# Two scan layers of a state-space stack: Softplus, step size products and their stores moved to later slots, GpSimd's units of B to other slots

## The chip, the core and the metric

The kernel runs on one core of a Trainium2 chip. Its engines are TensorE (PE in the profile), VectorE (DVE), ScalarE (ACT) and GpSimd (POOL); SyncE (SP) issues all transfers. Each engine works through its own queue in order. The metric is the device time of one execution in microseconds, the median over several runs.

## The reference

Four layers are applied to an image batch x of shape (8, 48, 48, 96), each as x = x + layer(group_norm(x)). Layer 1 is a band-limited quadratic MLP. Layers 0, 2 and 3 hold a selective scan: with 192 channels and 16 states, along the 2304 pixels in four directions in layers 0 and 3, and along single rows or columns of 48 pixels in layer 2. Layers 0 and 3 compute, per direction,

```python
dts, Bs, Cs = jnp.split(x_dbl, [R, R + N], axis=2)
dts = jnp.einsum('bkrl,kdr->bkdl', dts, dt_projs_weight)
delta = jax.nn.softplus(dts + dt_projs_bias...)
def step(h, inp):
    u, dl, Bv, Cv = inp
    dA = jnp.exp(dl[..., None] * A)
    h = h * dA + (dl * u)[..., None] * Bv[:, :, None, :]
    y = jnp.einsum('bkdn,bkn->bkd', h, Cv)
    return (h, y)
```

and then sum the four directions, normalise, gate with silu(z) and project back.

## The kernel before, in words

The layers run as `ss2d("l0")`, `lines` and `ss2d("l3")`. The MLP of layer 1 is a "guest": its pieces are put between the others' work while `l0` and `lines` run. The two calls of `ss2d` are called the scan layers here, the first and the last one.

**Blocks, slots, turns.** A scan layer has 8 images (jobs), 4 directions (two in row order, two in column order; they run in the order 0, 1, 3, 2) and 5 blocks of pixels, so 20 blocks a job and 160 a layer. Four blocks of a direction have ten rows (480 pixels, called full), one has eight (384). A block is worked off in 8 slots, and two slots make a turn; turns are counted 0 to 3. A slot holds one half of the channels and four of the 16 states, spread over 128 partitions and 3 units along the free axis. `ORDER` gives slots 0 to 3 the first half of the channels and slots 4 to 7 the second half, with the groups of states in reverse; so slots 3 and 4 use the same rows of B and C.

**What one unit needs.** `make_da` (L329) is the exponential of step size times A, on ScalarE, two units at a time, into one of two PSUM tiles `da`. `make_dbu` (L305) multiplies the products step size times u by B. `scan` (L337) is the recurrence, two units at a time, on VectorE. `make_hc` (L343) multiplies the three units of a slot by C on GpSimd, and `reduce` (L363, L365) sums over the states on TensorE.

**Who multiplies by B.** `on_pool` gives per slot how many of the three units GpSimd takes (the last ones, with B from SBUF); VectorE takes the others, with B copied to PSUM by ScalarE in `copy_b` (L286), a single buffer. Where GpSimd has all three units no copy is made. Where slot 3 has a copy, slot 4 shares it.

**The order of a turn.** The loop over turns issues, on every engine's queue, in this order: scan of pair 0; product with C of the slot before; VectorE's B products of slot at+2; exponentials of pair 1; GpSimd's B products of slots at+2 and at+3; reduction; scan of pair 1; exponentials of pair 2; copy of B and VectorE's B products of slot at+3; reduction; `aside(at)`; product with C of the turn's first slot; exponentials for the next turn's pair 0; scan of pair 2; copy of B of slot at+4; `aside(at + 1)`. So each B product is made a turn before its scan: slot 0 and 1 of the next block in turn 3.

**Asides.** `aside(at)` issues the loads and the work of `stage1` that are due at a slot. For block b, counted in slots from the start of the block two before it, `stage1` does: projection to the raw step sizes, B and C; their copy to `bcl` (L724) at slot 1; at slot 3 the store of B and C and the matrix product of the step sizes (L709); at slots 4 and 5 the biased step sizes of the two halves (L713), written to `dds`, a tile with one buffer; then Softplus over both halves in one instruction (L737, with a table load before it and another before the next exponential), the products step size times u on GpSimd (`make_du`, L505, with two small memsets), and per half a store of `dds` to device memory (`store_dd`, L491). In the block before b, the load of each half, replicated to 128 partitions (`load_dd`, L258), stands at slots 3 and 5, and the loads of B and C (`load_bc`, L270) at slots 1, 1, 6 and 7. A load of a half waits for that half's store. L713 of the next block waits for both stores.

In `lines` the corresponding steps are others: Softplus stands in the slot 0, and the products and both stores in slot 1, of the block before; the change does not touch it.

**Other work.** The asides also hold the side work of a scan layer (convolution of the next image with its Silu pairs, L593 and L595; normalisation and output of the image before, L609 to L659) and, in the first scan layer and `lines`, the guest.

Of the kernel before, what the change touches and what calls it, by code (L numbers as in the profile page):

```python
# [29 lines left out]
NG = 8  # L30
# [14 lines left out]
FAR = 1e30  # L45
CH = 96

ON_POOL_SS = {2: 1, 3: 3, 5: 1, 6: 1, 7: 3}
ON_POOL_L2 = {4: 3, 6: 3, 7: 3}


# [51 lines left out]
def vss_stack_kernel(ctx: ExitStack, tc: tile.TileContext, i: dict, out: bass.AP):  # L103
# [386 lines left out]
    def store_dd(b, half):  # L490
        nc.sync.dma_start(b.dd[half].rearrange("j (g m) -> g j m", g=3), b.dds[:, half].rearrange("p t m -> p (t m)"))  # L491

    def sizes(b, half):

        return [b.dds[:, half, n, b.at] for n in range(2)]

    def make_room(b, pools):
        b.room = pools["dds"].tile([DH, LEAD + 4 * WMAX], F32, tag="dds", name="dds")
        b.dds = b.room[:, LEAD:LEAD + 4 * b.m].rearrange("p (h t m) -> p h t m", h=2, t=2)

    def make_du(b, u):


        dt, du = [b.dds[:, :, n, b.at].rearrange("p h (r s) -> p h r s", s=SEG) for n in range(2)]
        nc.gpsimd.tensor_mul(du, dt, u)  # L505
        if b.m == b.n:
            at = SEG - 1 if b.rev else 0
            nc.gpsimd.memset(dt[:, :, :, at:at + 1], FAR)
        else:

            far = b.dds[:, :, :, b.came:] if b.back else b.room[:, :4 * b.m].rearrange("p (u m) -> p u m", m=b.m)[:, :, :LEAD + 1]
            nc.gpsimd.memset(b.dds[:, :, :, 0:1] if b.back else b.dds[:, :, :, b.goes:], 0.0)
            nc.gpsimd.memset(far, FAR)


    def ss2d(l, xin, xout, guest=None):
# [185 lines left out]
        def stage1(b):  # L702
            n = b.n
            u, uall = b.view(us[b.job], dirs[b.k][0]), b.view(uss[b.job], dirs[b.k][0])
            got = {}

            def raw(half):
                got["p"] = ps("s1", 1)
                nc.tensor.matmul(got["p"][:, :n], lhsT=wide("dtw", (2 * b.k + half) * DH), rhs=b.bcl[:, :n],  # L709
                                 start=True, stop=True)  # L710

            def biased(half):
                nc.scalar.activation(sizes(b, half)[0], got["p"][:DH, :n], AF.Identity,  # L713
                                     bias=w[f"{l}_dtb"][:, b.k, half:half + 1])

            def s0():
                got["p"] = ps("s1", 1)
                for half in range(2):
                    nc.tensor.matmul(got["p"][:, :n], lhsT=wide("xp", (2 * b.k + half) * NBC), rhs=uall[:, half],  # L719
                                     start=(half == 0), stop=(half == 1))  # L720

            def s1():
                b.bcl = pools["bcl"]
                nc.scalar.copy(b.bcl[:NBC, :n], got["p"][:NBC, :n])  # L724

            def s3():
                nc.sync.dma_start(b.bcd, b.bcl[:2 * NS, :n])
                raw(0)

            def s4():  # L730
                make_room(b, pools)
                biased(0)
                raw(1)

            def s6():
                both = b.dds[:, :, 0, b.at]
                nc.scalar.activation(both, both, AF.Softplus)  # L737

            def du():
                make_du(b, u)  # L740

            def store(half):
                return lambda: store_dd(b, half)

            return {-1: s0, 1: s1, 3: s3, 4: s4, 5: lambda: biased(1), 6: s6, 7: du,
                    NG: store(0), NG + 1: store(1)}

        def so_far(b, half):
            if b.job not in yss:
# [19 lines left out]
        for _ in conv(0, BLKS[:1]):  # L769
            pass  # L770
        scans(dirs, (0, 1, 3, 2), False, ON_POOL_SS, a, pools, ps, stage1, opening, done, side, tail, conv(0, BLKS[1:3]), guest)
        for _ in post(nb - 1, BLKS[:1]):
            pass
# [581 lines left out]
```

## Time and profile before

| | us |
|---|---|
| median of 3 runs | 17278.24 |
| lowest, highest | 17277.93, 17287.99 |
| profiled execution, its time | 17276.01 |
| profiled execution, its span | 17274.2 |

The profile comes from one execution. Its page gives busy time by engine and by group of instructions; the waits name, for the idle time of an engine, the instruction that waited and what it waited for; the timeline lists instructions with start and duration. A row of a group reads: line, engine, operation, output<-inputs, shape, count, then total busy us and mean ns of one, then the idle time before them and its main cause. SPq is SyncE's queue. By layer, in us of busy time:

| stretch | length | PE | DVE | ACT | POOL |
|---|---|---|---|---|---|
| first scan layer, 0 to 5909 | 5909 | 4635.0 | 5241.6 | 4684.1 | 5165.8 |
| `lines`, 5909 to 11854 | 5945 | 4497.7 | 5368.8 | 4921.7 | 4934.8 |
| last scan layer, 11854 to 17274 | 5420 | 3949.9 | 5186.2 | 4291.6 | 5087.6 |

### The profile page before, as it was taken

To read this page: it belongs to the slowest core of one execution; us is meant where nothing else is said; L and a number is where in the kernel's file an instruction comes from. 1 tells how busy PE (TensorE), PEld (TensorE's weight loads), DVE (VectorE), ACT (ScalarE), POOL (GpSimd) and SP (SyncE) were. 2 spreads that over 40 slices of the span, in tenths; PEclk is the share of its full clock that TensorE was granted. 3 is DMA by queue.
4 is the path that set the end of the run, shared out by engine and by line. 5 is a ranking of instruction groups with operands and counts; after the bars stand their busy time and mean duration, and the time that the engine had idled before them with its cause. 6 is when DMAs were issued, how large, how long until landed. Compare 5 with 4: busy or idle time off the path is not lost.

```text
span 17274.2 us, 168621 instructions
## 1 busy us (share of the span) xinstructions
PE 13082.7 (76%) x53740; PEld 4691.8 (27%) x53740; DVE 15796.7 (91%) x9680; ACT 13897.4 (80%) x20972; POOL 15188.2 (88%) x7999
## 2 busy tenths in 40 slices
PE   6778787878787677777777777776777777777776
PEld 1223232333332333233323332221222222222221
DVE  7999999998899799999999999996999999999998
ACT  6878888878787688888888888885878878878876
POOL 7998888988889688888888888887999999999998
PEclk7878888888898789899889998887878878878877
DMA  4555555454555444444444444443545455555454
GB/s 140 177 174 169 177 167 182 168 178 169 171 174 174 134 152 160 162 159 155 156 163 156 158 162 153 156 154 126 176 172 175 173 172 173 175 173 180 168 176 145
DMA packets 887917, 2843.64 MB, mean 165 GB/s; under 512 B 353469, under 2 KB 421789, under 8 KB 760207
## 3 DMA queue, kind: packets, MB, share of 16 engines
q1 hardware_dynamic: 887022, 2832.85, 48.3%
q8 instruction: 423, 6.93, 0.2%
q14 instruction: 472, 3.86, 0.1%
HBM read 2384.40 MB, written 448.17 MB: 164 GB/s over the span
## 4 chain that ended last, share of the span: by engine, by line
ACT 22%; POOL 21%; DVE 19%; issue 15%; DMA 13%; PE 9%; SPq 1%; POOLq 0%; DVEq 0%; ACTq 0%
POOL dbu L343 13%; DVE dbu L337 12%; ACT ps_da L329 8%; DMA dd<-dds 6%; DVE dbu L305 6%; POOL dbu L305 5%; DMA dd<-dd 4%; ACT L329 3%; POOL dds L505 3%; PE ps_y L363 2%; ACT ps_b L286 2%; DMA bc<-bcd 1%; PE ps_side L580 1%; ACT L737 1%; PE ps_s L709 1%
## 5 line engine op out<-in xcount | busy, mean ns | idle before, releaser
L337 DVE TENSOR_TENSOR_SCAN dbu<-ps_da,dbu 128x968 f32<-128x968 f32 (+3 forms) x5760 | 11826.1, 2075 | 889.5 <-ACT ps_da L329 725.5
L343 POOL TENSOR_TENSOR dbu<-dbu,bc 128x1440 f32<-128x1440 f32 (+1 forms) x3840 | 10071.2, 2635 | 1709.2 <-DVE dbu L337 1133.6
L329 ACT ACTIVATE ps_da<-dd,w_l_a 128x484 f32<-128x484 f32 (+3 forms) x11520 | 7417.2, 649 | 2337.4 <-DVE dbu L337 2108.6
L363 PE MATMUL ps_y<-dbu,w_red 128*32 128x480 f32 (+1 forms) x23040 | 4261.4, 656 | 1676.9 <-POOL dbu L343 1643.4
L365 PE MATMUL ps_y<-dbu,w_red 128*32 128x480 f32 (+1 forms) x7680 | 4222.1, 656 | 0.0
L305 DVE TENSOR_TENSOR dbu<-dd,ps_b 128x962 f32<-128x962 f32 (+5 forms) x2720 | 3815.4, 1403 | 318.1 <-ACT ps_b L286 164.0
L305 POOL TENSOR_TENSOR dbu<-dd,bc 128x481 f32<-128x481 f32 (+3 forms) x2080 | 3883.8, 1883 | 4.2 <-DMA bc<-bcd 4.1
L363 PEld LDWEIGHTS ps_y<-dbu,w_red 128*32 128x32 f32 x23040 | 717.6, 118 | 5117.2 <-POOL dbu L343 3585.2
L286 ACT COPY ps_b<-bc 128x482 f32<-128x482 f32 (+3 forms) x2720 | 1449.2, 533 | 270.3 <-DVE dbu L305 211.8
L580 PE MATMUL ps_side<-xpad,w_l_cw 128*128 128x480 f32 (+1 forms) x2880 | 1352.9, 608 | 47.4 <-ACT g_room L1181 17.3
L329 ACT ACT_TABLE_LOAD x993 | 1274.0, 1283 | 17.5
L709 PE MATMUL ps_s<-bcl,square 128*128 128x480 f32 (+1 forms) x1280 | 874.7, 774 | 325.9 <-ACT dds L713 170.8
L359 PE MATMUL ps_y<-big,eye 128*128 128x480 f32 (+1 forms) x960 | 745.0, 865 | 247.1 <-ACT big L760 242.4
L719 PE MATMUL ps_s<-big,square 128*128 128x480 f32 (+1 forms) x1280 | 848.8, 794 | 64.2 <-ACT g_room L1181 18.3
L505 POOL TENSOR_TENSOR dds<-dds,big 96x960 f32<-96x960 f32 (+1 forms) x320 | 706.5, 2208 | 144.5 <-ACT dds L737 144.0
L580 PEld LDWEIGHTS ps_side<-xpad,w_l_cw 128*128 128x128 f32 x2880 | 571.2, 209 | 808.9 <-issue 695.1
L872 PE MATMUL ps_sb<-xpad,square 128*128 128x480 f32 (+1 forms) x1280 | 615.7, 628 | 96.7 <-ACT g_room L1181 42.1
L365 PEld LDWEIGHTS ps_y<-dbu,w_red 128*32 128x32 f32 x7680 | 655.9, 118 | 0.0
L872 PE MATMUL ps_sa<-xpad,square 128*128 128x480 f32 (+1 forms) x1280 | 521.2, 548 | 0.0
L713 ACT ACTIVATE dds<-ps_s,w_l_dtb 96x480 f32<-96x480 f32 (+1 forms) x640 | 405.2, 633 | 126.1 <-DMA dd<-dds 81.3
L760 ACT COPY big<-ps_y 96x480 f32<-96x480 f32 (+1 forms) x640 | 471.7, 737 | 37.3 <-PE ps_y L365 35.9
L915 PE MATMUL ps_sa<-xpad,square 128*128 128x480 f32 (+1 forms) x320 | 243.5, 854 | 322.8 <-ACT g_room L1181 108.9
(250 smaller groups left out, 12475.6 us busy)
## 6 DMA issues: line engine op xcount, KB each, us to landing
dd<-dd SPq DMA_DIRECT2D x512, 1452.0 KB
bc<-bcd SPq DMA_DIRECT2D x1536, 480.0 KB
dd<-dd SPq DMA_DIRECT2D x256, 1440.0 KB
dd<-dds SPq DMA_DIRECT2D x512, 363.0 KB
dd<-dd SPq DMA_DIRECT2D x128, 1164.0 KB
bc<-bcd SPq DMA_DIRECT2D x384, 384.0 KB
dd<-dds SPq DMA_DIRECT2D x256, 360.0 KB
dd<-dd SPq DMA_DIRECT2D x64, 1152.0 KB
```

What stands on the lines that cost most here:

```text
L286: nc.scalar.copy(bps[t][:, :bcs[t][0].shape[1]], bcs[t][0])
L305: engine.tensor_mul(o, du, by.unsqueeze(1).to_broadcast([P, hi - lo, by.shape[1]]))
L329: nc.scalar.activation(da[:, at:at + b.m], b.got[half][:, u % 3, 0, :], AF.Exp, scale=a[:, b.k, ci:ci + 1])
L337: nc.vector.tensor_tensor_scan(db, da, db, 0.0, ALU.mult, ALU.add)
L343: nc.gpsimd.tensor_mul(h, h, bcs.pop(2 * t + sub)[1].unsqueeze(1).to_broadcast([P, 3, n]))
L363: nc.tensor.matmul(y[32 * g:32 * g + 32, :n], lhsT=wc["red"][:, :32], rhs=hc[:, g, b.at], start=False, stop=(slot == 3))
L365: nc.tensor.matmul(y[DH:, :n], lhsT=wc["red"][:, 32:], rhs=hc[:, 2, b.at], start=False, stop=(slot == 3))
L505: nc.gpsimd.tensor_mul(du, dt, u)
L580: nc.tensor.matmul(pu[:, :n], lhsT=flat[:, at:at + P], rhs=xpad[:, r0 + dy:r0 + dy + nr, dx:dx + W], start=(tap == 0), stop=(tap == 8))
L709: nc.tensor.matmul(got["p"][:, :n], lhsT=wide("dtw", (2 * b.k + half) * DH), rhs=b.bcl[:, :n], start=True, stop=True)
L719: nc.tensor.matmul(got["p"][:, :n], lhsT=wide("xp", (2 * b.k + half) * NBC), rhs=uall[:, half], start=(half == 0), stop=(half == 1))
L872: nc.tensor.matmul(got["u", half][:, :n], lhsT=wide("cw", at), rhs=shifted(off), start=(tap == 0), stop=(tap == 3))
```

## The change

Two edits, both for the scan layers alone. In `ON_POOL_SS` the three units of slot 3 and the one unit of slot 2 become three units of slot 1 and one of slot 3. In `stage1` Softplus moves from slot 6 to slot 0 of the block after (`NG` is 8), the products from slot 7 to slot 1 of it, and both stores stand right behind the products, where they stood at slots 0 and 1.

```diff
-ON_POOL_SS = {2: 1, 3: 3, 5: 1, 6: 1, 7: 3}
+ON_POOL_SS = {1: 3, 3: 1, 5: 1, 6: 1, 7: 3}
 ON_POOL_L2 = {4: 3, 6: 3, 7: 3}
...
             def du():
                 make_du(b, u)
-
-            def store(half):
-                return lambda: store_dd(b, half)
-
-            return {-1: s0, 1: s1, 3: s3, 4: s4, 5: lambda: biased(1), 6: s6, 7: du,
-                    NG: store(0), NG + 1: store(1)}
+                for half in range(2):
+                    store_dd(b, half)
+
+            return {-1: s0, 1: s1, 3: s3, 4: s4, 5: lambda: biased(1), NG: s6, NG + 1: du}
```

The instruction counts of the multiplies by B stay as they are on both engines: 15 units a block on VectorE in six instructions, 9 on GpSimd in five. The copies of B fall from six to five a block.

## The prediction

> **What bounds the kernel now.** I read the engine totals first, then the waits of each scan layer, then one block on the timeline of each engine.
>
> ```profile
> PE 13082.7 (76%) x53740; PEld 4691.8 (27%) x53740; DVE 15796.7 (91%) x9680; ACT 13897.4 (80%) x20972; POOL 15188.2 (88%) x7999
> L337 DVE TENSOR_TENSOR_SCAN dbu<-ps_da,dbu 128x968 f32<-128x968 f32 (+3 forms) x5760 | 11826.1, 2075 | 889.5 <-ACT ps_da L329 725.5
> ```
>
> VectorE is nearly full. By windows it is busy 5241.6 of the first scan layer's 5909.0 us and 5186.2 of the last one's 5420.0, so what can be won in these two layers is less than 667 + 234 us. The waits say what part of it ScalarE causes: 297.0 us in the first layer and, in the last one,
>
> ```profile
> DVE dbu L337 <- ACT ps_da L329: 84.5, 105, 3.4
> ```
>
> The transfers cost VectorE next to nothing there, but SyncE's queue waits for them all the time (last layer):
>
> ```profile
> SPq L258 <- DMA dd<-dds: 1563.5, 290, 6.6
> ```
>
> This is the load of the step sizes behind their store. One full block of the last layer, VectorE and then SyncE's queue:
>
> ```profile
> 13061.30 2.17 DVE L337 TENSOR_TENSOR_SCAN dbu<-ps_da,dbu 128x968 f32<-128x968 f32 x1 [1.03 <-ACT ps_da L329]
> 13063.39 1.13 DVE L305 TENSOR_TENSOR dbu<-dd,ps_b 128x962 f32<-128x962 f32 x1
> 13064.43 6.29 DVE L337 TENSOR_TENSOR_SCAN dbu<-ps_da,dbu 128x968 f32<-128x968 f32 x3
> ...
> 13087.37 1.63 DVE L305 TENSOR_TENSOR dbu<-dd,ps_b 128x1443 f32<-128x1443 f32 x1
> 13088.92 2.16 DVE L337 TENSOR_TENSOR_SCAN dbu<-ps_da,dbu 128x968 f32<-128x968 f32 x1
> 13091.00 1.63 DVE L305 TENSOR_TENSOR dbu<-dd,ps_b 128x1443 f32<-128x1443 f32 x1
> 13092.55 4.25 DVE L337 TENSOR_TENSOR_SCAN dbu<-ps_da,dbu 128x968 f32<-128x968 f32 x2
> ```
>
> ```profile
> 13061.48 0.74 SPq L491 DMA_DIRECT2D dd<-dds  x1
> 13062.27 2.15 SPq L270 DMA_DIRECT2D bc<-bcd  x2
> 13064.47 1.98 SPq L491 DMA_DIRECT2D dd<-dds  x1
> 13072.29 0.53 SPq L258 DMA_DIRECT2D dd<-dd  x1
> ```
>
> Times below count from the block's first scan (13061.30). The first store leaves at 0.2, the load that waits for it at 11.0, and VectorE first reads the loaded tile at 26.1 (13087.37, slot 0 of the next block). The next block starts at 33.4. So the chain store, load, product has slack now: the trace's landings put the load's end at 21.7 here (13082.95), 4.4 us early; over the layer's full blocks the median slack is 3.3.
>
> The middle layer, which is not changed, already does what the change brings: products and both stores at slot 1.
>
> ```profile
> 8001.32 1.55 SPq L491 DMA_DIRECT2D dd<-dds  x2
> 8010.92 0.56 SPq L258 DMA_DIRECT2D dd<-dd  x1
> ...
> 8015.71 0.55 SPq L258 DMA_DIRECT2D dd<-dd  x1
> 8020.22 1.66 DVE L305 TENSOR_TENSOR dbu<-dd,ps_b 128x1440 f32<-128x1440 f32 x1 [0.81 <-DMA dd<-dd]
> ```
>
> There the product waits for the load. Store to first use is 18.9 us here; from the first store's issue to the load's last landing the median over that layer's full blocks is 18.4.
>
> **GpSimd's units of B.** VectorE's and GpSimd's counts do not change: 9 units a block on GpSimd, 15 on VectorE, in multiplies of the same three widths. Two things do. Slot 3 now has a copy of B in PSUM and slot 4 shares it, and slot 1 needs none: 320 fewer copies (L286, 0.53 us) in all, 170 us of ScalarE, which is no bound. And VectorE's multiplies move: turn 0 gets slot 2's third unit (1.63 - 1.13 = 0.50) and slot 3's two (1.05 back to back), turn 3 loses slot 1's three (1.55). So the first use of the loaded tile moves from 26.1 to 27.6, and from it to the block's end there remain 7.28 - 1.55 = 5.73 us.
>
> **Softplus.** The same 3.6 us (table 1.28, activation 1.01, table 1.28) goes from turn 3 to turn 0. There VectorE has 8.9 us of scans and multiplies; ScalarE has its copy at 4.4, Softplus done by 6.7, the exponentials of the next turn by 9.3 against a need at 8.9. About even, so I take 0; if its cover is gone (a Silu burst of 3.8 in the same turn) it costs up to 2.9. The page "ScalarE: Activation LUTs" of the Trainium skill, section "What ACT_TABLE_LOAD costs", prices a switch at 2.66 us with its drain. By that the burst would be an estimated 6.3 us and each block 2.7 us longer; the trace of this case shows the activation 0.02 us behind a load of 1.28, so I do not use it.
>
> **Products and stores.** They now follow Softplus in the same turn, and on GpSimd they stand behind slot 0's product with C (L343), which needs VectorE's second scan. That scan ends at 5.2 now and at 5.7 after; 2.72 for L343 makes 8.5; the product and its memsets took 2.17 (13093.85 to 13096.02) in row order: the store leaves at 10.7, as in the middle layer. In column order the product takes 2.70 instead of 1.88 (the group of 256 has a mean of 2.29): 11.5. Before it was 0.2 to 1.4. The stores lose some 10 us of lead; the use is only 1.5 later.
>
> With 18.4 the load lands at 29.1 in row order and 29.9 in column order, against 27.6. VectorE stalls 1.5 and 2.3 us, at the one place where it has nothing else queued. GpSimd's new units of slot 1 wait for the same load, but GpSimd gets there only at about 28 to 30, so nothing is added. Since VectorE then starts the next block late, and the stores hang on that block's second scan, this is a loop: a full block can't be shorter than 29.1 + 5.73 = 34.8 (35.6 in column order), where the block shown takes 33.4.
>
> Why a store takes so long decides all this. The trace's landings show three engines' worth of completions for it, and two stores one behind the other: first landed 9.6 us after issue, second at 14.4. The page "DMA: Bandwidth & Descriptors", section "Why a DMA increments its semaphore by 16 and not by 1", says that a transfer's engines are the largest number up to 16 that divides the slowest dimension on both sides; with 3 and 96 that is 3, which fits. The same page's fit in "Anatomy of one DMA" (2.0 us plus bytes at 436 GB/s) speaks against a stall: 2.8 us for 363 KB and 5.3 for the load, an estimate of 18.8 for the landing, 9 us early, and the sum would be no loss. The rows here say 9.6, and they decide.
>
> **Where dds is written next.** The tile has one buffer. The biased step sizes of the following block (L713) wait for both stores. Now they come at 20.2 (ScalarE's timeline, 13081.53) and wait 38.9 us in the whole last layer; after, they come at 21.8 and the tile is free at 10.7 + 14.4 = 25.1. ScalarE stands for 3.3 us in each block, and behind it stand the exponentials of turn 3, and on TensorE the next projection (L709) and the reductions. The exponentials are there at 25.1 + 0.64 + 1.37 = 27.1, so the scan that should run from 25.5 ends at 29.2, just when the load lands: the two delays overlap and are paid once. Bounds for what is added: 0 when they overlap wholly; 320 x 3.3 = 1056 us when nothing covers the wait. ScalarE is idle 21% of the last layer, about 7 us a block, so I stay near the lower end: 0.4 us a block for bursts that find no room, 128 us. SyncE waits in order for GpSimd's product; behind it are the loads of dd, then the store of B and C and the last two loads of B and C, which have 10 us or more to spare as in the middle layer.
>
> **Sum.** A job has 20 blocks: 13 full ones behind a full one (7 row, 6 column), 3 behind one of eight rows (floor 32.4 to 33.2 against 30.8), one short behind short (+2.4), 3 without loss: 33 us a job, 266 us in the last layer if every block were at its median. Many are longer already (mean 34.5, median 33.3). Taking for each block the larger of its own length in the trace and its floor gives +155 us in the last layer, and in the first, where the median full block takes 35.7, +53. With the 128: 336. ScalarE's 170 us earn nothing in blocks that are set by the load. 17276 us for the profiled execution (span 17274.2) + 336 = 17612, and the median of the runs is 2 higher: 17614.
>
> **Rivals.**
> 1. ScalarE and TensorE jam: the wait at L713 is not covered. For it: in the first layer TensorE is busy 78% and also serves the guest layer, and in-order queues pass on every wait. Against it: the 7 us of idle time. If a third of 3.3 us gets through on top in 320 blocks: +350, 17960.
> 2. Faster. The place is Softplus in turn 3, where ScalarE also had two copies; VectorE's 297 + 85 us of waiting for exponentials would halve: -190, 17090. It decides only if the load lands before 27.6, which needs store to landing under 16.9 us; the middle layer has 18.4, and three engines are three engines. Against it also the 3.3 us at L713.
> 3. Near the edge: without the loads of B and C between the stores they land 1.5 us sooner than in the middle layer; only column blocks stall, and the relief pays part: +80, 17360.
>
> **Numbers.** Forecast 0.57, jam 0.2, edge 0.13, faster 0.1. A measurement of this kernel can tell 0.2%, some 35 us, from no change. Faster by more: 0.09; within: 0.05 (the low end of the edge case); slower: 0.86. The forecast's own range is 17,450 to 17,800; 8 in 10 reach from the edge case to the jam: 17,330 to 17,960.
>
> **What would show it.** Right: a new wait of VectorE's L305 for dd in both scan layers, 1 to 2 us a block; L713 waiting for the stores some 3 us a block; stores issued 10.7 to 11.5 after a block's first scan; full blocks of the last layer at 34.8 to 36; the middle layer at its 5945 us. Wrong: the load's landing before 27.6, or stores that land in less than 9 us; waits for ScalarE growing in turn 0 instead would mean that Softplus, not the load, is what was moved into the way.

## The result, and the profile after

The changed kernel takes 18153.1 us (median of 5 runs, 18137.2 to 18169.5) against 17280.9 us before in the same runs: a ratio of 1.050, with a 95% interval of 1.049 to 1.052. It is 872 us slower where 336 were forecast. The direction and the place were right, the size was not.

Engine totals and three groups of the page of the changed kernel (busy us and mean ns, then idle time before the group and its main cause):

```profile
PE 13157.0 (72%) x53740; PEld 4799.0 (26%) x53740; DVE 15851.6 (87%) x9680; ACT 13760.4 (76%) x20653; POOL 15208.8 (84%) x7999
...
L337 DVE TENSOR_TENSOR_SCAN dbu<-ps_da,dbu 128x968 f32<-128x968 f32 (+3 forms) x5760 | 11863.8, 2077 | 1436.7 <-ACT ps_da L329 1156.7
...
L305 DVE TENSOR_TENSOR dbu<-dd,ps_b 128x962 f32<-128x962 f32 (+5 forms) x2720 | 3823.1, 1406 | 575.7 <-DMA dd<-dd 282.0
...
L713 ACT ACTIVATE dds<-ps_s,w_l_dtb 96x480 f32<-96x480 f32 (+1 forms) x640 | 408.0, 638 | 869.3 <-DMA dd<-dds 764.2
```

VectorE does the same work (15,852 us against 15,797) and waits more. The share named "DMA" before L305 is 282 us, but the waits must be read together: L713 on ScalarE waits 764 us for the stores (before: 81), and what VectorE then waits for exponentials (1157 against 725) is partly that wait handed on. From the first scan of a layer to the first scan of the next (in the last layer: of its last block), the first scan layer went from 5793 to 6272 us, the middle one from 5946 to 5937, the last one from 5359 to 5767: +479, -9, +408. The granted clock of TensorE fell from 0.85 to 0.83, but VectorE's waits for TensorE's side work grew by little (L657: from 55 to 73 us in the first scan layer and from 51 to 58 in the last), too little to be a rival.

The block that the prediction showed, in the changed kernel; it starts at 13617.1. SyncE's queue first:

```profile
13627.80 1.64 SPq L491 DMA_DIRECT2D dd<-dds  x2
13637.70 0.56 SPq L258 DMA_DIRECT2D dd<-dd  x1
...
13642.58 0.56 SPq L258 DMA_DIRECT2D dd<-dd  x1
13643.19 11.25 SPq L270 DMA_DIRECT2D bc<-bcd  x4
```

ScalarE's two rows of the biased step sizes:

```profile
13642.63 0.66 ACT L713 ACTIVATE dds<-ps_s,w_l_dtb 96x480 f32<-96x480 f32 x1 [2.49 <-POOL dbu L305]
...
13645.42 0.66 ACT L713 ACTIVATE dds<-ps_s,w_l_dtb 96x480 f32<-96x480 f32 x1
```

And VectorE at the end of the block:

```profile
13644.58 2.17 DVE L337 TENSOR_TENSOR_SCAN dbu<-ps_da,dbu 128x968 f32<-128x968 f32 x1 [0.64 <-ACT ps_da L329]
13647.35 1.66 DVE L305 TENSOR_TENSOR dbu<-dd,ps_b 128x1443 f32<-128x1443 f32 x1 [0.60 <-ACT ps_da L329]
13648.93 6.29 DVE L337 TENSOR_TENSOR_SCAN dbu<-ps_da,dbu 128x968 f32<-128x968 f32 x3
```

The stores leave 10.7 us after the first scan. The second one has landed at 25.4 (13642.53). Right behind it the second load leaves (13642.58), and ScalarE's L713 starts (13642.63), which stood for 2.49 us; the releaser that the profile names is a GpSimd instruction, but the start follows the store's landing by 0.1 us. The trace has the first load's landing at 13647.23, and VectorE's product starts at 13647.35; here too the row names another releaser, an exponential. The next block starts at 13653.1: 35.9 us where it took 33.3.

### The profile page after: what moved, and what is told of

Its sections match the earlier page's. It is cut to its first block, busy times and chain, and to the rows that moved or that the text cites. A ratio compares the mean times of both kernels' runs of the same rounds, so it can differ in the third digit from the quotient of the medians.

```text
span 18151.3 us, 168013 instructions
## 1 busy us (share of the span) xinstructions
PE 13157.0 (72%) x53740; PEld 4799.0 (26%) x53740; DVE 15851.6 (87%) x9680; ACT 13760.4 (76%) x20653; POOL 15208.8 (84%) x7999
## 4 chain that ended last, share of the span: by engine, by line
DMA 30%; ACT 19%; POOL 14%; DVE 14%; issue 12%; PE 10%; SPq 2%; POOLq 0%; DVEq 0%; ACTq 0%
DMA dd<-dds 16%; DVE dbu L337 9%; POOL dbu L343 8%; DMA dd<-dd 8%; ACT ps_da L329 6%; DVE dbu L305 4%; DMA bc<-bcd 4%; ACT L329 3%; POOL dds L505 3%; POOL dbu L305 2%; PE ps_y L363 2%; ACT ps_b L286 1%; PE ps_side L580 1%; DMA out_dram<-xi 1%; ACT L737 1%
## 5 line engine op out<-in xcount | busy, mean ns | idle before, releaser
L363 PE MATMUL ps_y<-dbu,w_red 128*32 128x480 f32 (+1 forms) x23040 | 4183.2, 654 | 1127.4 <-POOL dbu L343 1122.0
L305 DVE TENSOR_TENSOR dbu<-dd,ps_b 128x962 f32<-128x962 f32 (+5 forms) x2720 | 3823.1, 1406 | 575.7 <-DMA dd<-dd 282.0
L305 POOL TENSOR_TENSOR dbu<-dd,bc 128x481 f32<-128x481 f32 (+3 forms) x2080 | 3895.5, 1883 | 302.8 <-DMA dd<-dd 192.0
L365 PE MATMUL ps_y<-dbu,w_red 128*32 128x480 f32 (+1 forms) x7680 | 4148.0, 654 | 0.0
L363 PEld LDWEIGHTS ps_y<-dbu,w_red 128*32 128x32 f32 x23040 | 761.7, 120 | 4469.9 <-POOL dbu L343 2615.2
L286 ACT COPY ps_b<-bc 128x482 f32<-128x482 f32 (+3 forms) x2400 | 1284.8, 535 | 558.1 <-DMA bc<-bcd 358.8
L709 PE MATMUL ps_s<-bcl,square 128*128 128x480 f32 (+1 forms) x1280 | 932.2, 821 | 1068.0 <-ACT dds L713 885.2
L359 PE MATMUL ps_y<-big,eye 128*128 128x480 f32 (+1 forms) x960 | 784.5, 909 | 431.6 <-ACT big L758 425.2
L713 ACT ACTIVATE dds<-ps_s,w_l_dtb 96x480 f32<-96x480 f32 (+1 forms) x640 | 408.0, 638 | 869.3 <-DMA dd<-dds 764.2
L365 PEld LDWEIGHTS ps_y<-dbu,w_red 128*32 128x32 f32 x7680 | 695.6, 120 | 0.0
L709 PEld LDWEIGHTS ps_s<-bcl,square 128*128 128x128 f32 x1280 | 263.9, 252 | 1598.2 <-ACT dds L713 1193.9
L870 PE MATMUL ps_sa<-xpad,square 128*128 128x480 f32 (+1 forms) x1280 | 521.2, 548 | 0.0
```

Of the source, the lines that this page charges most:

```text
L286: nc.scalar.copy(bps[t][:, :bcs[t][0].shape[1]], bcs[t][0])
L305: engine.tensor_mul(o, du, by.unsqueeze(1).to_broadcast([P, hi - lo, by.shape[1]]))
L363: nc.tensor.matmul(y[32 * g:32 * g + 32, :n], lhsT=wc["red"][:, :32], rhs=hc[:, g, b.at], start=False, stop=(slot == 3))
L365: nc.tensor.matmul(y[DH:, :n], lhsT=wc["red"][:, 32:], rhs=hc[:, 2, b.at], start=False, stop=(slot == 3))
L870: nc.tensor.matmul(got["u", half][:, :n], lhsT=wide("cw", at), rhs=shifted(off), start=(tap == 0), stop=(tap == 3))
```

## The experiments

Eight kernels ran; each was timed beside the kernel before. The ratios are to the kernel before.

**The units alone.** The kernel before with one line changed:

```diff
-ON_POOL_SS = {2: 1, 3: 3, 5: 1, 6: 1, 7: 3}
+ON_POOL_SS = {1: 3, 3: 1, 5: 1, 6: 1, 7: 3}
```

> The kernel before with the changed kernel's units of B alone; Softplus, products and stores stay at slots 6, 7, 8 and 9. The load lands as early as before (about 22 us after a block's first scan), so both the theory of the load and that of the wait at the biased step sizes expect no loss: 17,150 to 17,350. A theory that the units themselves cost the time (VectorE's turn 3 is 1.55 us shorter and no longer covers Softplus; GpSimd's three units of slot 1 in turn 3) expects 0.6 to 2 us a block, 17,450 to 17,900.

Measured: 17522.2 us, 1.014 (1.013 to 1.016). Slower by 240 us, within what the third theory expected and not what the first two did, although the load is early (landed 24.7 us after the first scan, needed at 27.7, medians of the last layer's full blocks). The units are no gain by themselves: with Softplus left in turn 3, that turn has only 7.8 us of VectorE's work to cover it and takes 8.6. VectorE's scans wait 167 us for exponentials in the last layer (before: 85) and 397 in the first (before: 297), while their wait for GpSimd's products with C hardly changes in the last layer (28 against 26), so of the two causes that the third theory named the waits show the first.

**The stage alone.** The changed kernel with the old line for the units.

> The kernel before with Softplus, products and stores moved, the units of B as before. The theory of the load: the loop keeps its landing (30.3 us after the first scan in the last layer), but 7.28 instead of 5.73 us of VectorE's work stand behind it, so a block is 1.5 us longer than in the changed kernel: 18,150 + 480 = 18,600, at least 18,400. If the units were the cause of the loss it would be gone: below 17,500.

Measured: 18643.7 us, 1.079 (1.077 to 1.081); the theory of the load said 18,600. So the units are not the cause of the loss; they save 490 us of what the moved stage costs.

**Two buffers of dds in the last layer.** Memory allows it there alone, since the guest's tiles are gone by then; in the first layer this wasn't tried.

```diff
-                 "dds": pool("dds", 1),
+                 "dds": pool("dds", rooms),
...
-        pools, ps = scan_pools(stack)
+        pools, ps = scan_pools(stack, 1 if guest else 2)
```

> The changed kernel with two buffers of dds in the last scan layer alone, so that the biased step sizes there wait for no store. Theory of the load: it lands as before, the last layer stays within 60 us of its 5831, the whole at 18,090 to 18,170. Theory of the wait at the biased step sizes: the last layer loses 150 us or more, the whole is below 18,000.

Measured: 18154.2 us, 1.051 (1.049 to 1.052), with the last layer at 5759 us against 5767. The wait at L713 is gone and nothing is won. The end of the same block on VectorE shows why (timeline):

```profile
13651.57 6.29 DVE L337 TENSOR_TENSOR_SCAN dbu<-ps_da,dbu 128x968 f32<-128x968 f32 x3
13659.76 1.66 DVE L305 TENSOR_TENSOR dbu<-dd,ps_b 128x1443 f32<-128x1443 f32 x1 [1.89 <-DMA dd<-dd]
13661.33 6.30 DVE L337 TENSOR_TENSOR_SCAN dbu<-ps_da,dbu 128x968 f32<-128x968 f32 x3
```

The scans that came late now run in one go, and VectorE waits 1.89 us for the load instead. In the last layer's waits the load takes the first place, with 314 us where the changed kernel showed 67. The changed kernel first, then this one:

```profile
DVE dbu L337 <- ACT ps_da L329: 309.7, 289, 4.6
...
DVE dbu L305 <- DMA dd<-dd: 66.7, 56, 3.9
```

```profile
DVE dbu L305 <- DMA dd<-dd: 314.1, 113, 6.3
DVE dbu L337 <- ACT ps_da L329: 120.5, 186, 4.4
```

**Quick stores in the changed kernel.** Each store is cut into three transfers of 32 rows.

```diff
-        nc.sync.dma_start(b.dd[half].rearrange("j (g m) -> g j m", g=3), b.dds[:, half].rearrange("p t m -> p (t m)"))
+        for g in range(3):
+            nc.sync.dma_start(b.dd[half].rearrange("j (g m) -> g j m", g=3)[g],
+                              b.dds[32 * g:32 * g + 32, half].rearrange("p t m -> p (t m)"))
```

> The changed kernel with each store split into three transfers of 32 rows, one for each group of 32 partitions; in all three scan layers. If a store is slow because its outer dimension of 3 puts it on three engines, it lands in 3 to 5 us instead of 9.7. Theories of the load and of the wait at the biased step sizes alike: the load lands at about 21 us, both waits of dds are gone, 17,100 to 17,400. A theory that Softplus in turn 0 is what costs the time (exponentials late for turn 1): stays above 17,700. If the stores land as late as before, 18,100 and nothing is learned but that.

Measured: 17144.3 us, 0.992 (0.991 to 0.994). SyncE's queue in the same block, which starts at 12948.6:

```profile
12959.26 2.63 SPq L492 DMA_DIRECT2D dd<-dds  x6
12962.26 0.52 SPq L258 DMA_DIRECT2D dd<-dd  x1
...
12965.65 0.52 SPq L258 DMA_DIRECT2D dd<-dd  x1
```

The load of the first half leaves 3.0 us after the first of the six transfers, where it was 9.9. Each transfer lands about 2.0 us after its issue, the load lands at 20.9 us after the first scan (last layer, median) and is needed at 28.2. The two scan layers together take 11141 us against 12039 with the slow stores: 898 us of the changed kernel are the stores' path.

**Quick stores in the kernel before.** The same edit there.

> The kernel before with the split stores, in all three scan layers. Its two scan layers had 3 us of slack at the load and should not change (5793 and 5359 us from the first to the last block's first scan); the middle layer, which stands at its load, should win as it did with the changed kernel, about 110 us: 17,130 to 17,200. If it comes out as after_16 (17,144), the parts of the change are worth nothing once the stores are quick; if it is above 17,250, they are worth something.

Measured: 17063.0 us, 0.988 (0.986 to 0.989), less than expected and the fastest of all kernels here. The middle layer goes from 5946 to 5830 us; the first and the last one also win a little, 5734 and 5333 against 5793 and 5359, which was not expected. Against this kernel the changed one with quick stores is 81 us slower, so the two edits are worth nothing, and cost a little, once the stores are out of the way (82 us more in the first scan layer, 7 less in the last). Of the 887 us that the change added to the two scan layers 74 remain so, and 813 hang on the slow stores.

**The stage alone with quick stores.**

> stage_only with the split stores: Softplus in a turn 0 in which VectorE has 7.3 us of work instead of 8.9. With the store path out of the way, what is left is ScalarE's burst: exponentials for turn 1 at about 9.3 us against a need at 7.3, 1 to 2 us a block in 320 blocks, less the 0 to 1.1 that turn 3 gets back: 17,250 to 17,700. If the units are needed for nothing but the stores' path: 17,150.

Measured: 17374.4 us, 1.006 (1.004 to 1.007), as expected of ScalarE's burst. Turn 0 of a block of the last layer on VectorE; the block's first scan is the second one of the first row, at 12261.1:

```profile
12259.01 4.23 DVE L337 TENSOR_TENSOR_SCAN dbu<-ps_da,dbu 128x968 f32<-128x968 f32 x2
12263.16 1.13 DVE L305 TENSOR_TENSOR dbu<-dd,ps_b 128x962 f32<-128x962 f32 x1
12264.21 4.23 DVE L337 TENSOR_TENSOR_SCAN dbu<-ps_da,dbu 128x968 f32<-128x968 f32 x2
12269.68 2.17 DVE L337 TENSOR_TENSOR_SCAN dbu<-ps_da,dbu 128x968 f32<-128x968 f32 x1 [1.24 <-ACT ps_da L329]
```

The first scan of turn 1 waits 1.24 us for its exponential, and turn 0 takes 8.6 us, as in the median over the layer's full blocks, where it takes 7.3 in the kernel before with quick stores. This wait has nothing to do with a store: the load lands at 21.4 us and is needed at 27.6 (medians). Units alone cost 256 us in the two scan layers (11408 against 11152), the stage alone with quick stores 321 (11388 against 11067 of the kernel before with quick stores), both with quick stores 74: each edit needs the other, since VectorE's work has to stand where Softplus stands. The units alone were not run with quick stores; their load is 3.0 us early in the median as it is.

**Only the second half's store quick.**

```diff
+        if half == 0:
+            nc.sync.dma_start(b.dd[half].rearrange("j (g m) -> g j m", g=3), b.dds[:, half].rearrange("p t m -> p (t m)"))
+            return
+        for g in range(3):
...
```

> The changed kernel with the store of the second half alone split. The first half's store still takes 9.7 us, so the load of the first half leaves at 21 as before. Theory that this load is slowed by the second store, which stands before it on three engines: it takes 6.6 us instead of 9.2, lands at 28 us after the first scan, where VectorE needs it at 28.2, and most of the loss is gone: 17,250 to 17,500. Theory that only the first store's 9.7 us matter: the load lands at 30 as before, 18,000 to 18,150.

Measured: 17390.6 us, 1.007 (1.005 to 1.008), as the first theory said. SyncE's queue in the same block, which starts at 13105.2 (L492 is the slow store, L495 the three quick ones):

```profile
13115.89 0.74 SPq L492 DMA_DIRECT2D dd<-dds  x1
13116.68 3.94 SPq L495 DMA_DIRECT2D dd<-dds  x3
13125.33 0.54 SPq L258 DMA_DIRECT2D dd<-dd  x1
```

The first load leaves 9.4 us after its store, nearly as in the changed kernel, but it lands 6.7 us after that instead of 9.2 (medians, last layer), at 27.3 against a need at 28.2. With the second store quick 763 of the 1009 us that two quick stores win are gone already. Part of this came through the first half's load, which stands behind the second store; the run does not separate it from the store's own later landing, for which L713 and the second load wait.

**Products ahead of GpSimd's product with C.** In the changed kernel `make_du` moves to slot 0, right behind Softplus; the stores stay at slot 1.

> The changed kernel with the products right behind Softplus at slot 0, ahead of GpSimd's product with C; both stores stay at slot 1. Theory of the loop (first scan, products, store, load, next block): products start at 6.7 instead of 8.5 us in the last layer, and some 0.5 to 1 us earlier in the first, where Softplus itself is later; every block that stands at its load gets shorter by that: 290 + 80 to 160 us less, 17,700 to 17,850. If the loss is not set by when the stores leave, 18,100 or more.

Measured: 17844.9 us, 1.033 (1.032 to 1.035): 308 us faster than the changed kernel, as the loop asks, though less than the 370 to 450 that were expected: the last layer won 199 us instead of 290, the first one 92, within its 80 to 160. The stores leave at 9.5 us in the last layer (11.0 in the changed kernel) and 10.7 in the first (11.5).

Medians over the full blocks of the last layer that are followed by a full block, in us from the block's first scan; the landings are the trace's, "needed" is the end of turn 3's first scan:

| kernel | block | store leaves | load leaves | load landed | needed | turns 0 to 3 |
|---|---|---|---|---|---|---|
| before | 33.3 | 1.4 | 12.2 | 22.9 | 26.2 | 7.3, 9.4, 7.3, 9.3 |
| changed | 36.4 | 11.0 | 21.2 | 30.3 | 30.3 | 9.3, 9.5, 8.8, 8.8 |
| two buffers of dds | 36.3 | 10.8 | 21.2 | 30.3 | 28.2 | 9.3, 9.5, 7.3, 10.3 |
| products at slot 0 | 34.9 | 9.5 | 19.3 | 28.4 | 28.6 | 9.3, 9.5, 7.3, 8.4 |
| second store quick | 34.3 | 11.1 | 21.0 | 27.3 | 28.2 | 9.3, 9.5, 7.3, 7.8 |
| both stores quick | 33.8 | 10.8 | 14.4 | 20.9 | 28.2 | 9.3, 9.5, 7.3, 7.8 |

## Why the prediction was wrong

**Right.** The mechanism: the stores leave 11.0 us after the first scan in the last layer (10.7 to 11.5 forecast), the load that hangs on them sets the block, and the next block's stores hang on that. With quick stores 898 us of the two scan layers go, where the change had added 887; against the kernel before with the same stores 813 of the 887 go. Also right: the wait at L713 and the load end together and are paid once; with two buffers in the last layer the block only swaps a turn 2 of 8.8 for a turn 3 of 10.3. This is also why the first sign came out small: VectorE's wait for dd is 67 us in the last layer, 0.4 a block instead of 1 to 2, and with two buffers 314, 2.0 a block. The middle layer stayed (5937 against 5946). The first rival, a jam of ScalarE and TensorE on top, had a number nearer to the result, but as a cause in the last layer it falls with the two buffers there: taking the wait away won 8 us. So that layer's half of the 128 us that the sum held for L713 was not there either. In the first layer this was not tried. The faster rival needed the load to land before 27.6; it landed at 30.3. The third rival's condition names no difference, since the middle layer's rows show no loads of B and C between its stores either.

**The step that failed** is the sum's "Taking for each block the larger of its own length in the trace and its floor", which gave 155 us in the last layer and 53 in the first, where 408 and 479 were measured. The floor in it was too low, and the rule itself misses a part. How much is which can be estimated from the traces. For the full blocks that are followed by a full block, the rule with the forecast's floors gives 123 us in the last layer and 50 in the first, and these blocks grew by 268 and 278. With the lengths that the shortest quarter of them took after the change (36.3 and 37.5 us, below) as floors the same rule gives 222 and 196. So about two thirds of what is missing there is the floor and one third the rule. The other blocks, those of eight rows and those ahead of one, grew by another 140 and 200 us.

**The floor was too low.** 34.8 and 35.6 were forecast for both layers; the median in the last one is 36.4. The load landed at 30.3 instead of 29.1 to 29.9. From the first store's issue to the landing it is 19.4 us and not the 18.4 of the middle layer: the load takes 9.2 against 8.6 there, the store 9.7 against 9.6, and SyncE issues the load on average 0.5 us behind its store's landing against 0.1. Why the load takes longer than in the middle layer was not tried. Behind the landing 5.8 us follow in the median and 6.4 on average, not 5.7. In the first layer the store leaves at 11.5 (in a tenth of the blocks later than 14.4), the load lands at 31.1, and the block takes 38.1.

**The rule misses a part** because it supposes that a block which is long already hides the load. I sorted the full blocks that are followed by a full block of the same image by their length before. In the last layer the shortest quarter grew by 3.2 us, from 33.1 to 36.3 on average, and the longest still by 2.4, from 37.2 to 39.6; in the first layer by 3.9 (33.6 to 37.5) and 1.5 (39.9 to 41.4). The long blocks' excess stands in turn 0 and in turn 3 (9.0 and 10.9 us on average in the longest quarter of the last layer, against 7.3 and 9.3 in the shortest), and turn 3 is still 10.4 there after the change. What stands in turn 3 behind the load's first use comes on top of it, and what stands in turn 0 ahead of the second scan delays the stores as well: after the change the stores leave at 12.0 in the longest quarter and at 11.2 in the shortest, and 7.7 against 5.9 us follow the load's landing (averages, last layer).

**Softplus at 0** held for the last layer and not for the first. With quick stores on both sides the last layer takes 5325 us against 5333 and the first one 5816 against 5734. In the median the sum of the turns is 33.8 against 33.3 us in the last layer and 35.6 against 34.6 in the first, where turn 0 takes 10.7 us against 8.9 of VectorE's work. Its cover is thinner there than the row of the last layer said; VectorE's wait for exponentials in that layer is 342 us with the change and 272 without it, both with quick stores.

**SyncE's queue** did not have 10 us to spare. The last two loads of B and C stand behind the second load of dd, and ScalarE's copies of B waited for them, in the first layer

```profile
ACT ps_b L286 <- DMA bc<-bcd: 206.3, 91, 8.3
```

against 16.2 us before. With quick stores it is 37.5. VectorE itself waited 68 us there for these copies, below 9 before and 14 with quick stores; what this is worth in time was not tried by itself.

## What to carry to other kernels

A step that is moved takes the start of its transfers with it: measure from the issue of the store to the last landing of the load that waits for it, and hold that against the distance in time to the first use, not against the engines' busy time. If a loop of latencies becomes the longest path, take each of its links from the place where it will run: here the load, SyncE's wait and the stretch behind the landing were each a little longer than in the rows they were taken from. Idle time that stands in the loop's own links adds to it; taking the larger of the two block by block is only right for idle time that lies beside the path, and here it missed an estimated third. And before work is moved about to hide a slow transfer, look at how many engines carry it: here one transfer cut into three gave 1.2% (0.988, 0.986 to 0.989) in the kernel before, more than either order of the work.

## What the runs showed of the hardware that was not expected

A store of 363 KB whose outer dimension is 3 took 9.7 us, and a second one issued 0.8 us later landed 14.6 us after the first one's issue (last layer, medians). The same bytes as three transfers of 32 rows landed about 2.0 us after issue each, all six within 4.4 us. The Trainium skill, "DMA: Bandwidth & Descriptors", section "Why a DMA increments its semaphore by 16 and not by 1", lets 3 engines carry the first and 16 the others, and the trace agrees: a slow store has three late completions (8.0, 8.3 and 9.7 us after its issue), a quick transfer sixteen. The quick transfers (121 KB) agree with that page's fit in "Anatomy of one DMA", an estimate of 2.3 us; the slow store does not, at 2.8 against 9.7. The page gives this fit for transfers that GpSimd issues, and the stores here are issued by SyncE.

A load over all engines waits for the slow store ahead of it: it took 9.2 us behind the second slow store and 6.7 when that store was quick, with nothing else changed. Its completions show where: behind the slow store fifteen of the sixteen come by 6.9 us and the last at 9.0; behind the quick one all sixteen come by 6.6 (medians, last layer). In the run with only the second store quick, the first of its three transfers stands behind the slow store, and thirteen of its completions come by 2.1 us, the other three at 7.4 to 9.0: only three engines were held up.
